# Cross-attention on one core: where the third part of product 5 is kept, and in which order GpSimd's queue takes the last batch's transfers

## The chip, the core and the metric

The kernel runs on one core of a Trainium2 chip. The core has five engines that work through their own instruction queues in order: TensorE (PE) multiplies matrices into PSUM, VectorE (DVE) adds, subtracts and scales, ScalarE (ACT) copies out of PSUM and computes exponentials, GpSimd (POOL) here reduces over the 128 partitions and issues transfers that add onto their destination, and SyncE (SP) issues plain transfers. Sixteen DMA engines carry the transfers of all queues. The metric is the device time of one execution in microseconds, as the median of a few runs; lower is better. The largest and the smallest of the runs shown lie 1.7 us apart.

## The reference

For each of 8 batches, with x1 and x2 of 512 channels by 1024 positions:

```python
q = jnp.einsum('bcn,dc->bnd', x1, Wq) + bq                # 64 wide
k = jnp.einsum('bcn,dc->bdn', x2, Wk) + bk[:, None]
v = jnp.einsum('bcn,dc->bdn', x2, Wv) + bv[:, None]
attn = jax.nn.softmax(jnp.einsum('bnd,bdm->bnm', q, k), axis=2)
attn_out = jnp.einsum('bcm,bnm->bcn', v, attn)
return attn_out + x1
```

The inputs are 32-bit floats. There is no mask: every position of x1 looks at every position of x2.

## The kernel before

The kernel does not form v. It first multiplies the unnormalised attention with x2 (stage "y"), scales by the softmax's denominators, and then multiplies with Wv (stage "o"); bv and x1 are added at the end. Both stages are products of two by two blocks, done with seven block products instead of eight. The products are numbered 1 to 7 as in the table `MULT`; their left factors are blocks or sums of blocks of x2 (`s.a`), their right factors blocks or sums of blocks of the exponentials (`s.t`: "11", "12", "21", "22", T1, T2, T3, T4). Most products of stage y are themselves done with seven smaller ones: `multiply_seeded` runs these as seven steps in the order 1, 7, 6, 2, 5, 4, 3, each of which the profile shows as four matmuls. Its steps 1, 6, 5 and 4 go through a PSUM chain (`ps_i5chain` for product 5) from which ScalarE copies into the result's banks, and step 7 makes the "third" part (`ps_i5third`), which ScalarE copies into an SBUF buffer `v` (L640). At the end `complete` adds `v` to the second bank on VectorE (L655). Which buffer `v` gets is the third argument of the call, the tag of a pool.

Tags with one buffer are shared by tiles whose lives are meant not to overlap. Two are of concern. "r" holds the output block "12" of a batch (the tile's name begins with r, as does that of block "11", which lies in "u1"), from the biased copy out of PSUM (L743) through the adding transfer of x1 onto it (L755) to the write-out (L756). "top" has two buffers used in turn. It holds the maxima over the keys of one half of the positions (L274), which VectorE subtracts before the exponential (L323); `multiply_seeded` also uses it for `v` where it is told to, and in the last batch wherever "r" is named (L633).

The program is one long list in an order written out by hand; `period(s, n, nn, nnn)` emits the work of batch `s`, interwoven with the scores, maxima and exponentials of the next batch `n` and the projections of the one after, `nn`. Batches are counted from 0 in the code. Batches 2 to 5 are "six" batches (`s.six`), with product 6 done in seven steps too; batches 1, 6 and 7 are not, and batch 0 has a branch of its own. In the last batch `n` is None.

In batches from 1 on the order of the stretch touched by the change is: product 1, VectorE's sums T1 and T2, two adding transfers that make T3 in place, the leaving of the previous batch's last outputs (x1 added by a GpSimd-issued transfer, then SyncE's write-out), product 2, the sum over half 1 (`total_1`: VectorE sums, GpSimd's reduction over partitions L293, a small transfer `few`), the eviction of y11, the inverse of half 0's denominators. In batches 1, 6 and 7 follow T4 = T2 - T21 (`copy_t4`: ScalarE negates; `add_t4`: two transfers on GpSimd's queue add T2), then product 6, in the not-last batches the next batch's scores and the queries of the one after, and product 5 with the eviction of the queries (`evict_q`) hooked behind its step 6. `shares(s, 1)` sends half 1's inverse denominators: a reciprocal on VectorE, a small transfer `row` to DRAM (L303), and a transfer that spreads it over the partitions (L308), both on GpSimd's queue. Products 7, 3 and 4 follow; product 4 reads T4, first through `inner_right` (L526 to L533), then through TensorE.

Batch 6 leaves two outputs for batch 7 to send: block "22" in the buffer "u5" and block "12" in "r". Stage o of batch 7 copies its own product 5 into "u5" as well (`multiply_57`, L579 and L594).

Of the kernel before, what the change touches and what calls it, by code (L numbers as in the profile page):

```python
# [15 lines left out]
def kernel(  # L16
# [270 lines left out]
    def total_1(s):  # L287
        sum_1(s)
        reduce_total(s, 1)
# [9 lines left out]
    def invert(s, h):  # L299

        nc.vector.reciprocal(s.few[h], s.few[h])
        s.row[h] = row = dram.tile([1, H], F32, tag="row", name=f"row_{s.b}_{h}")
        nc.gpsimd.dma_start(row.rearrange("o (p f) -> (o p) f", p=P), s.few[h])  # L303

    def spread(s, h):

        s.rden[h] = s.den[h]
        nc.gpsimd.dma_start(s.rden[h], s.row[h].broadcast_to([P, H]))  # L308

    def shares(s, h):  # L310
        invert(s, h)
        spread(s, h)
# [7 lines left out]
    def lower(s, h, i):  # L320
        e = s.e[h][:, :, i, :]
        top = s.top[h].unsqueeze(1).to_broadcast([P, 2, H])
        nc.vector.tensor_tensor(e, e, top, ALU.subtract)  # L323
# [26 lines left out]
    def copy_t4(s, parts=(0, 2)):  # L350

        if parts[0] == 0:
            s.t["T4"] = sb.tile([P, MH, H], F32, tag="eT4", name=f"eT4_{s.b}")
        t4 = s.t["T4"]
        for i in parts:
            nc.scalar.mul(t4[:, i : i + 2, :], s.t["21"][:, i : i + 2, :], -1.0)

    def add_t4(s):

        t4 = s.t["T4"]  # L360
        for i in (0, 2):
            nc.gpsimd.dma_start(t4[:, i : i + 2, :], s.t["T2"][:, i : i + 2, :], accum_op=ALU.add)

    def sum_t3(s, i):

        t3 = s.t["T3"][:, i : i + 2, :]
        nc.gpsimd.dma_start(t3, s.t["22"][:, i : i + 2, :], accum_op=ALU.add)
# [6 lines left out]
    def copy_u1(s, j):  # L374
        if j == 0:
            s.tmp[1] = sb.tile([P, 2, H], F32, tag="y22" if s.six else "yT1", name=f"uy1_{s.b}")
        nc.scalar.copy(s.tmp[1][:, j, :], s.bank["a", j])
# [118 lines left out]
    def weave(*streams):  # L496

        streams = list(streams)
        while streams:
            for stream in list(streams):  # L500
                if next(stream, "end") == "end":
                    streams.remove(stream)

    def left_stream(s, i, x, tag):

        v = {f"{p + 1}{q + 1}": x[:, ts(q, MH // 2), ts(p, P)] for p in range(2) for q in range(2)}
        sums = sb.tile([P, 4, MH // 2, P], F32, tag=tag, name=f"aI{i}_{s.b}")
        s.inner[i] = v
        for z, (k, x, y, op) in enumerate(LEFT):
            v[k] = sums[:, z]  # L510
            nc.vector.tensor_tensor(v[k], v[x], v[y], op)  # L511
            yield
# [4 lines left out]
    def right_stream(s, i, x, *tags):  # L517

        half = x.shape[1] // 2
        v = {f"{q + 1}{r + 1}": x[:, ts(q, half), ts(r, H // 2)] for q in range(2) for r in range(2)}  # L520
        last = 4 // len(tags)
        shape = [P, last, half, H // 2]
        sums = [sb.tile(shape, F32, tag=t, name=f"eI{i}{t}_{s.b}") for t in tags]
        both, t2, t4 = sums[0][:, 0:2], sums[-1][:, last - 2], sums[-1][:, last - 1]
        part = x.rearrange("p (q k) (r n) -> p q k r n", q=2, r=2)
        nc.vector.tensor_tensor(  # L526
            both, part[:, :, :, 1, :], part[:, 0].rearrange("p k r n -> p r k n"), ALU.subtract
        )
        s.inner[i, "t"] = v | {"T1": both[:, 0], "T3": both[:, 1], "T2": t2, "T4": t4}
        yield  # L530
        nc.vector.tensor_tensor(t2, both[:, 0], v["22"], ALU.subtract)
        yield
        nc.vector.tensor_tensor(t4, v["21"], t2, ALU.add)  # L533
        yield

    def inner_right(s, i, x, *tags):
        weave(right_stream(s, i, x, *tags))
# [83 lines left out]
    def multiply_seeded(s, i, v_tag, hooks={}, bank=None):  # L621

        bank = bank or MULT[i][2]

        def fresh(j):
            s.bank[bank, j] = ps = ps_a.tile(
                [P, H], F32, tag=f"{bank}{j}", name=f"ps_y{bank}{j}_{s.b}_{i}"
            )
            return ps

        b0 = fresh(0)
        chain, third = inner_parts(s, i)
        if v_tag == "top" or s.b == B - 1 and v_tag == "r":  # L633
            v = sb.tile([P, H], F32, tag="top", name=f"v{i}_{s.b}", bufs=2)[:, left]
        else:
            v = sb.tile([P, 2, H], F32, tag=v_tag, name=f"v{i}_{s.b}")[:, 0, left]
        def step(z, ps, opens, out=None, of=None):
            inner_product(s, i, z, ps, opens)
            if out is not None:
                nc.scalar.copy(out, of)  # L640
            if z in hooks:
                hooks[z]()

        step(1, chain, True, b0[:, left], chain)
        step(7, third, True, v, third)
        b1 = fresh(1)
        step(6, chain, False, b1[:, left], chain)
        step(2, b0[:, left], False)
        step(5, chain, False, b0[:, right], chain)
        step(4, b1[:, left], False, b1[:, right], chain)  # L650
        step(3, b0[:, right], False)

        def complete(b1=b1):
            b = b1.rearrange("p (a n) -> p a n", a=2)
            nc.vector.tensor_tensor(b, b, v.unsqueeze(1).to_broadcast([P, 2, H // 2]), ALU.add)  # L655

        return complete
# [249 lines left out]
    def period(s, n, nn, nnn):  # L907

        late = s.b >= 1
        five = late and nn is not None  # L910

        def first(i, rows=range(2)):
            multiply(s, "y", i, s.a, s.t, MH, rows=rows)
# [19 lines left out]
        def scores_0():  # L933
            then = scores_and(n, 0, 1 if nn else 2, "c", next_queries if nn else nothing)
            if nn is None:
                first(6, (1,))
            if s.six:
                copy_u6(s, 0)
                copy_u6(s, 1)
                nc.gpsimd.dma_start(s.tmp[6], s.tmp[1], accum_op=ALU.add)  # L940
                add_t4(s)
                weave(folds(n, 0, "max", ALU.max), right_stream(s, 7, s.t["T3"], "yT1", "yT2"))
                highest(n, 0)
            elif s.b:
                weave(folds(n, 0, "max", ALU.max), right_stream(s, 7, s.t["T3"], "yT1", "yT2"))
                highest(n, 0)
            return then
# [70 lines left out]
        else:  # L1018
# [11 lines left out]
            if not early:  # L1030
                sum_t3(s, 0)
                sum_t3(s, 2)
            for leave in s.leave:
                leave()
            if n and not early:
                invert(s, 0)
            if s.six:
# [4 lines left out]
            if n is None:  # L1042
                weave(left_stream(s, 7, s.a["S3"], "yT4"))
            complete_2 = multiply_seeded(
                s, 2, "yT1" if s.six else "y22", {5: lambda: copy_u1(s, 0), 4: lambda: copy_u1(s, 1)}
            )
            if s.b > 1:
                total_1(s)
            complete_2()
# [5 lines left out]
            if s.six:  # L1055
                complete_6 = multiply_seeded(
                    s, 6, "top", {6: lambda: copy_t4(s, (0,)), 4: lambda: copy_t4(s, (2,))}
                )
            else:
                copy_t4(s)  # L1060
                add_t4(s)
                first(6, (0,) if n and nn is None else range(2))
            if n:
                weave(left_stream(s, 7, s.a["S3"], "yT4"))
# [6 lines left out]
            if n:  # L1071
                evict_q = scores_0()
                spread(s, 0)
            if n is None:
                weave(right_stream(s, 7, s.t["T3"], "yT1", "yT2"), left_stream(s, 3, s.a["S4"], "aI3"))
            complete_5 = multiply_seeded(
                s, 5, "r", {6: evict_q} if five else {}, "a"
            )
            complete_5()
            shares(s, 1)  # L1080
            if n:
                weave(right_stream(s, 3, s.t["22"], "eT1"), left_stream(s, 3, s.a["S4"], "aI3"))
                lower(n, 0, 0)
            else:
                inner_right(s, 3, s.t["22"], "eT1")
# [160 lines left out]
        leave = evict_o(s, "22")  # L1246
# [35 lines left out]
    with tc.manual_schedule():  # L1282
        head(states[0])
        for b in range(B):
            period(*states[b : b + 4])
# [31 lines left out]
```

## Time and profile before

| what | value |
|---|---|
| median of 3 runs | 682.67 us (682.05 to 683.75) |
| the profiled execution, its time | 684.36 us |
| the profiled execution, its span | 682.6 us |
| mean granted TensorE clock in it | 0.995 of full |
| packets on the DMA engines | 134.79 MB, mean 197 GB/s |

The span is the time from the first to the last instruction that the profile shows; the profiled execution takes 1.76 us more around it. All times within the run are counted from the start of the span. A timeline row has its start, the time it covers, the engine, the line of the kernel, the operation, the tiles (out<-in), their size and the count; in brackets stands the idle time of the engine before it and what ended it. A row of the list of waits has the total, the number of times and the longest.

### The profile page before, as it was taken

How to read it: one execution, taken by the hardware profiler on the slowest of the kernel's cores; microseconds unless marked ns; L12 is line 12 of the kernel's file. 1: busy time of each engine (PE TensorE's matmuls, PEld its weight loads, DVE VectorE, ACT ScalarE, POOL GpSimd, SP SyncE). 2: the span in 40 equal slices, each digit the busy share in tenths (PEclk: the TensorE clock that was granted, in tenths of full speed). 3: DMA queues.
4: the chain of work that ended last, by engine and by line, in shares of the span. 5: the costliest groups of instructions: out<-in, count | busy, mean ns of one | idle time of the engine just before them, and what ended most of it. 6: DMA issues, size and time to landing. Idle time of an engine off the chain costs nothing.

```text
span 682.6 us, 7705 instructions
## 1 busy us (share of the span) xinstructions
PE 668.1 (98%) x2558; PEld 425.3 (62%) x2558; DVE 607.1 (89%) x823; ACT 363.4 (53%) x636; POOL 226.8 (33%) x196
## 2 busy tenths in 40 slices
PE   9999999979999999999999999999999999999997
PEld 5334754737557685586656876566855767566854
DVE  1998899895989899897999989998999989989894
ACT  2754466424754556645655557556476346564321
POOL 0126214631145413443224631354223540145400
PEclk9999999997999999999999999999999999999999
DMA  9678587995499897998699985999959991688602
GB/s 300 270 204 266 164 232 139 196 238 182 108 254 217 191 262 187 225 208 224 189 252 207 220 229 163 276 200 224 261 102 210 196 311 49 123 139 187 154 31 108
DMA packets 51783, 134.79 MB, mean 197 GB/s; under 512 B 5664, under 2 KB 7968, under 8 KB 51744
## 3 DMA queue, kind: packets, MB, share of 16 engines
q0 software_dynamic: 24480, 61.94, 50.2%
q1 hardware_dynamic: 26976, 71.97, 29.6%
q10 hardware_dynamic: 288, 0.39, 0.2%
q8 instruction: 20, 0.33, 0.2%
q14 instruction: 19, 0.16, 0.1%
HBM read 86.77 MB, written 16.81 MB: 152 GB/s over the span
## 4 chain that ended last, share of the span: by engine, by line
PE 78%; DMA 11%; DVE 4%; POOL 2%; issue 2%; ACT 2%; SPq 0%; DVEq 0%; POOLq 0%; ACTq 0%
PE ps_yc L544 9%; PE ps_ya L544 6%; PE ps_s L238 5%; PE ps_oa L463 5%; PE ps_oa L585 5%; PE ps_o L463 4%; PE ps_o L483 4%; PE ps_oc L463 4%; PE ps_k L191 3%; PE ps_i4chain L544 3%; PE ps_q L191 3%; PE ps_i3chain L544 2%; DMA uo<-in_x_dram 2%; PE ps_i5chain L544 2%; PE ps_i7chain L544 2%
## 5 line engine op out<-in xcount | busy, mean ns | idle before, releaser
L293 POOL PARTITION_ALL_REDUCE den<-sum x16 | 53.4, 3340 | 75.9 <-DVE sum L268 75.9
L763 POOL DMA_DIRECT2D sum<-e x21 | 26.9, 1279 | 140.5 <-ACT sum L768 43.6
L323 DVE TENSOR_TENSOR e<-e,top 128x1024 f32<-128x1024 f32 x60 | 71.4, 1217 | 2.3 <-POOL top L274 2.3
L332 ACT ACTIVATE e<-e 128x1024 f32<-128x1024 f32 x60 | 62.7, 1056 | 12.1 <-DVE e L323 11.4
L274 POOL PARTITION_ALL_REDUCE top<-max x16 | 32.2, 2012 | 64.0 <-DVE max L268 42.4
L247 ACT COPY e<-ps_s 128x1024 f32<-128x1024 f32 x46 | 45.6, 1029 | 9.7 <-PE ps_s L238 7.0
L238 PE MATMUL ps_s<-q,k 64*128 64x512 f32 x188 | 47.6, 608 | 0.9 <-ACT q L790 0.8
L258 DVE TENSOR_TENSOR max<-max,e 128x1024 f32<-128x1024 f32 x30 | 36.5, 1216 | 0.2
L238 PEld LDWEIGHTS ps_s<-q,k 64*128 64x128 f32 x188 | 17.3, 186 | 22.5 <-issue 15.5
L640 ACT COPY ps_ya<-ps_i1chain 128x256 f32<-128x256 f32 x28 | 10.0, 358 | 36.9 <-PE ps_i1chain L544 33.4
L677 DVE TENSOR_TENSOR y<-y,den 128x1024 f32<-128x1024 f32 x24 | 29.2, 1234 | 0.2
L308 POOL DMA_DIRECT2D den<-row x16 | 8.9, 558 | 60.9 <-DMA row<-few 40.9
L755 POOL DMA_DIRECT2D r<-in_x_dram x14 | 28.5, 2033 | 1.0 <-ACT ps_yc L640 1.0
L463 PE MATMUL ps_oa<-yT,w_S 128*128 128x512 f32 x64 | 28.8, 592 | 0.0
L463 PE MATMUL ps_o<-y,w 128*128 128x512 f32 x64 | 28.8, 592 | 0.0
L483 PE MATMUL ps_o<-y,w 128*128 128x512 f32 x64 | 28.8, 592 | 0.0
L463 PE MATMUL ps_oc<-yT,w 128*128 128x512 f32 x64 | 28.8, 592 | 0.0
L640 ACT COPY ps_yc<-ps_i7chain 128x256 f32<-128x256 f32 x32 | 11.4, 357 | 31.2 <-PE ps_i7chain L544 25.2
L511 DVE TENSOR_TENSOR aI<-a,aI 128x256 f32<-128x256 f32 x60 | 25.2, 421 | 1.3
L640 ACT COPY ps_ya<-ps_i5chain 128x256 f32<-128x256 f32 x32 | 11.4, 358 | 27.8 <-PE ps_i5chain L544 22.9
L511 DVE TENSOR_TENSOR aI<-a 128x256 f32<-128x256 f32 x60 | 25.7, 449 | 0.0
L191 PE MATMUL ps_q<-x_in_x_dram,wqk_sb 128*64 128x512 f32 x112 | 25.6, 598 | 0.0
(282 smaller groups left out, 1788.4 us busy)
## 6 DMA issues: line engine op xcount, KB each, us to landing
x_in_x_dram<-in_x_dram SPq DMA_DIRECT2D x60, 512.0 KB, 8.9
a<-in_x2T_dram SPq DMA_DIRECT2D x32, 512.0 KB, 10.3
sum<-e POOLq DMA_DIRECT2D x21, 512.0 KB, 7.5
aS<-in_x2T_dram POOLq DMA_DIRECT2D x19, 512.0 KB, 10.4
eT<-eT POOLq DMA_DIRECT2D x16, 512.0 KB, 11.1
uo<-in_x_dram POOLq DMA_DIRECT2D x14, 512.0 KB, 10.1
r<-in_x_dram POOLq DMA_DIRECT2D x14, 512.0 KB, 11.3
e<-e POOLq DMA_DIRECT2D x14, 512.0 KB, 10.8
```

Of the source, the lines that this page charges most:

```text
L191: nc.tensor.matmul(ps[r, :], w_sb[:, c, :], s.x[:, c, ts(h, H)], start=(c == 0), stop=(c == CT - 1),)
L238: nc.tensor.matmul(ps[g], s.k[r, ts(i, P)], s.q[r, ts(h, H)], start=True, stop=True)
L247: nc.scalar.copy(e[:, :, i, :], whole)
L258: nc.vector.tensor_tensor(f, e[:, :, 0, :] if i == 1 else f, e[:, :, i, :], op)
L293: nc.gpsimd.partition_all_reduce(s.den[h], s.mx[h][:, 0, :], P, ReduceOp.add)
L323: nc.vector.tensor_tensor(e, e, top, ALU.subtract)
L332: nc.scalar.activation(e, e, AF.Exp)
L463: nc.tensor.matmul(ps[:, n], left[ka][:, k, ts(j, P)], right[kb][:, k, n], start=opens and k == 0, stop=i in (2, 3, 4) and k == n_k - 1, s ...
L483: nc.tensor.matmul(ps, w["11"][:, k, ts(j, P)], s.y["11"][:, k, :], start=k == 0, stop=False, skip_group_check=True)
L511: nc.vector.tensor_tensor(v[k], v[x], v[y], op)
L544: nc.tensor.matmul(ps, s.inner[i][ka][:, k, :], s.inner[i, "t"][kb][:, k, :], start=opens and k == 0, stop=z in (2, 3, 4) and k == n_k - 1 ...
L585: nc.tensor.matmul(ps[:, n], w[ka][:, k, ts(j, P)], s.y[kb][:, k, n], start=False, stop=i == 3 and k == 1, skip_group_check=True,)
```

## The change

Three edits. The third part of product 5 goes to the buffer tag "top" in the batches that are not "six" batches (1, 6 and 7; the last used "top" already). In the last batch, the negations and transfers of T4 are put between product 2 and the sum over half 1. And in the last batch the leaving of batch 6's outputs (both the transfers of x1 onto them and the write-outs) is put behind the sending of half 1's denominators.

```diff
-            for leave in s.leave:
-                leave()
+            if n:
+                for leave in s.leave:
+                    leave()
             if n and not early:
                 invert(s, 0)
...
             complete_2 = multiply_seeded(
                 s, 2, "yT1" if s.six else "y22", {5: lambda: copy_u1(s, 0), 4: lambda: copy_u1(s, 1)}
             )
+            if n is None:
+                copy_t4(s)
+                add_t4(s)
             if s.b > 1:
                 total_1(s)
...
             else:
-                copy_t4(s)
-                add_t4(s)
+                if n:
+                    copy_t4(s)
+                    add_t4(s)
                 first(6, (0,) if n and nn is None else range(2))
...
             complete_5 = multiply_seeded(
-                s, 5, "r", {6: evict_q} if five else {}, "a"
+                s, 5, "r" if s.six else "top", {6: evict_q} if five else {}, "a"
             )
             complete_5()
             shares(s, 1)
+            if n is None:
+                for leave in s.leave:
+                    leave()
```

The order of instructions changes on GpSimd's queue alone. In batch 7, behind the two transfers of T3, it was: x1 onto "u5", x1 onto "r", the reduction of half 1, `few` of half 1, `row` and the spread of half 0, T4's two transfers, `row` and the spread of half 1. It becomes: T4's two transfers, the reduction of half 1, `few` of half 1, `row` and the spread of half 0, `row` and the spread of half 1, x1 onto "u5", x1 onto "r". SyncE's write-outs keep their places, and wait for the x1 transfers as before.

## The prediction

> Batches are counted from 0 here, as in the code, so the title's batches 2 and 7 are batches 1 and 6, and the last is batch 7. Times within the run are microseconds of the profiled execution before the change.
>
> **What bounds the kernel now.** First the page's table of engines, then the list of what TensorE's matmuls waited for.
>
> ```profile
> PE 668.1 (98%) x2558; PEld 425.3 (62%) x2558; DVE 607.1 (89%) x823; ACT 363.4 (53%) x636; POOL 226.8 (33%) x196
> ```
> ```profile
> PE ps_i5chain L544 <- ACT ps_ya L640: 5.5, 1, 5.5
> ...
> PE ps_i4third L544 <- DVE eI4eT L526: 1.0, 1, 1.0
> ```
>
> TensorE (PE) is busy for 668.1 of 682.6 us, so the end moves only if TensorE waits less or runs faster. Inside the batches it has one long pause, before a step of product 5, and one of 1.0 us before a step of product 4. The timeline shows what each costs. The first three rows below are product 5 of batch 1 (its first step, the step behind the pause, the second step of product 7); the last two are the same first step and the same second step of product 7 in batch 6, which has no pause.
>
> ```profile
> 145.90 1.13 PE L544 MATMUL ps_i5chain<-eT,aS 128*128 128x256 f32 x4
> ...
> 155.08 2.08 PE L544 MATMUL ps_i5chain<-eI5y,aI 128*128 128x256 f32 x4 [5.46 <-ACT ps_ya L640]
> ...
> 161.44 1.03 PE L544 MATMUL ps_i7third<-eI7yT,aI 128*128 128x256 f32 x4
> ```
> ```profile
> 556.26 1.03 PE L544 MATMUL ps_i5chain<-eT,aS 128*128 128x256 f32 x4
> ...
> 563.16 1.03 PE L544 MATMUL ps_i7third<-eI7yT,aI 128*128 128x256 f32 x4
> ```
>
> The same eight steps take 161.44 - 145.90 = 15.54 us in batch 1 and 563.16 - 556.26 = 6.90 us in batch 6 (0.86 a step). The excess is 8.64 us, of which 5.46 is the pause; the rest, 3.18, is a slower clock, as the 2 us windows show (their first number after POOL's is the granted clock, the next the DMA engines' busy share).
>
> ```profile
> 154.00:156.00 2.00, 0.92 (x2) 0.84 (x3) 0.00 (x0) 1.60 (x4) 0.79 (x2) 0.50 1.03 394
> ...
> 160.00:162.00 2.00, 2.00 (x9) 1.69 (x8) 1.46 (x3) 0.31 (x1) 0.54 (x1) 0.80 0.91 213
> ...
> 164.00:166.00 2.00, 2.00 (x11) 1.74 (x11) 1.60 (x3) 0.40 (x2) 0.54 (x1) 1.00 0.00 0
> ...
> 174.00:176.00 2.00, 2.00 (x12) 0.77 (x8) 2.00 (x5) 2.00 (x3) 0.00 (x0) 1.00 0.00 0
> ```
>
> Behind the pause the clock is at half until somewhere past 160. Who made the pause stands on ScalarE (ACT) and on SyncE's queue (SP):
>
> ```profile
> 145.87 0.37 SPq L756 DMA_DIRECT2D out_dram<-r  x1
> ```
> ```profile
> 154.38 0.37 ACT L640 COPY v<-ps_i5third 128x256 f32<-128x256 f32 x1 [6.90 <-DMA out_dram<-r]
> ...
> 168.55 0.37 ACT L640 COPY v<-ps_i3third 128x256 f32<-128x256 f32 x1 [0.45 <-PE ps_i3third L544]
> ```
>
> The copy of product 5's third part waits 6.90 us, because its buffer "r" is still being written out for batch 0, a transfer issued at 145.87. ScalarE's later copies stand behind it in order, and TensorE needs those.
>
> **The change, part by part.** *Product 5 in batch 1.* The part goes to "top", the two buffers of the maxima, used in turn. The copy then takes the buffer of batch 1's maximum of half 1, and has to wait for that maximum alone, the first row below; the second is the next maximum, in the other buffer.
>
> ```profile
> 107.86 2.20 POOL L274 PARTITION_ALL_REDUCE top<-max  x1
> ...
> 144.17 4.13 POOL L293 PARTITION_ALL_REDUCE den<-sum  x1 [8.31 <-DVE sum L268]
> ...
> 152.57 1.77 POOL L274 PARTITION_ALL_REDUCE top<-max  x1 [3.38 <-DVE max L268]
> ```
>
> So it needs no wait: pause and half clock both go, **-8.64 us** (bounds: 5.46 if the clock were low anyway, 8.64). What becomes late next? Product 3's third part stays in "r" and inherits the wait. It stood at 168.55 and moves to 168.55 - 8.64 = 159.91; the write-out had landed by 154.38, 5.5 us earlier, so this costs nothing. The transfers in flight at the pause are over by 164 (DMA share 0.00), before the next keys' matmuls need their x at 176.39 - 8.64 = 167.75:
>
> ```profile
> 176.39 3.65 PE L191 MATMUL ps_k<-x_in_x_dram,wqk_sb 128*64 128x512 f32 x16
> ```
>
> VectorE (DVE) waited in this pause too, and its work now falls beside GpSimd's maximum at 152.57:
>
> ```profile
> 145.12 3.26 DVE L526 TENSOR_TENSOR eI7yT<-e 128x1024 f32<-128x1024 f32 x1
> ...
> 159.28 0.70 DVE L655 TENSOR_TENSOR ps_ya<-ps_ya,v 128x512 f32<-128x512 f32 x1 [6.82 <-ACT ps_ya L640]
> ...
> 160.60 1.22 DVE L526 TENSOR_TENSOR eI3eT<-e 128x1024 f32<-128x1024 f32 x1 [0.54 <-PE ps_ya L544]
> ```
>
> The form that takes 1.22 us took 3.26 beside GpSimd's sum at 144.17, so such company can cost 2.04. VectorE is free at 159.28 - 6.82 = 152.46; the first sum for product 3 starts 0.78 behind it (160.60 - 159.28, less the 0.54 idle) and takes 1.22, so it is ready by 154.5, or 156.5 with the 2.04 added. Product 3's second step, which reads it, starts one step ahead of its copy, 159.91 - 0.86 = 159.05. I take 0 (bounds 0 and 2.04). The Trainium skill, page "SBUF — State Buffer", section "SBUF: two separate sides", speaks against this change here: VectorE operations with two SBUF inputs and GpSimd exclude each other for the whole instruction. That would make the 2.04 likely, and still leave it covered by the slack just worked out.
>
> *Product 5 in batch 6* copies without waiting for the write-out already (the steps above run at 0.86), so 0; bounds 0 and 0.
>
> *The last batch.* T4 is -T21 by ScalarE plus T2 by a transfer. Before, the two transfers stand in GpSimd's queue behind half 1's sum, and behind the sending of half 0's denominators.
>
> ```profile
> 623.41 2.00 ACT L356 ACTIVATE eT<-e 128x1024 f32<-128x1024 f32 x2
> ```
> ```profile
> 620.84 1.85 POOL L755 DMA_DIRECT2D uo<-in_x_dram  x1
> ...
> 630.35 3.23 POOL L293 PARTITION_ALL_REDUCE den<-sum  x1 [6.44 <-DVE sum L268]
> ...
> 637.85 1.85 POOL L362 DMA_DIRECT2D eT<-eT  x2
> ```
> ```profile
> 637.99 0.17 DVE L301 RECIPROCAL few<-few 128x4 f32<-128x4 f32 x1
> ...
> 646.96 1.23 DVE L526 TENSOR_TENSOR eI4eT<-eT 128x1024 f32<-128x1024 f32 x1 [1.25 <-DMA eT<-eT]
> ```
> ```profile
> 646.32 1.03 PE L544 MATMUL ps_i4chain<-eT,a 128*128 128x256 f32 x4
> 648.33 1.10 PE L544 MATMUL ps_i4third<-eI4eT,aI 128*128 128x256 f32 x4 [0.98 <-DVE eI4eT L526]
> ```
>
> After, they wait for the negations, over at 623.41 + 2.00 = 625.41, and their two issues (1.85) are off GpSimd by 627.3, 3 us before the sum can start: the sum is not delayed, so bounds 0 and 0. Their landing, from the view of their line, is:
>
> ```profile
> L362 POOL DMA_DIRECT2D eT<-eT x16: 919/1250/2121, 62.7 to 638.4; - x16
> ...
> DMA to landing us min/median/max: 5.6/11.1/18.1
> ```
>
> Even 18.1 from the last issue (about 626.5) gives 644.6, ahead of VectorE's 646.96 - 1.25 = 645.71. VectorE gains 1.25, and TensorE's second step of product 4 starts at 646.32 + 0.86 = 647.18 instead of 648.33: **-1.15 us**. VectorE's chain to the end keeps its distance, since it moves by slightly more. Bounds 0 and 1.15.
>
> *The two x1 transfers onto batch 6's outputs* move from 620.84 past half 1's sum, both denominators' rows and both spreads, to GpSimd's last place; SyncE's two write-outs follow them, with batch 7's write-outs queued behind. The reader to fear is "u5": batch 7's own part of product 5 is copied into it.
>
> ```profile
> 665.80 0.59 ACT L594 COPY uo<-ps_oc 128x512 f32<-128x512 f32 x1 [4.56 <-PE ps_oc L585]
> ```
> ```profile
> DMA to landing us min/median/max: 1.7/6.7/14.1
> ```
> ```profile
> DMA to landing us min/median/max: 6.4/11.7/16.3
> ```
> ```profile
> DMA to landing us min/median/max: 2.7/8.5/11.2
> ```
>
> These three rows belong to the denominators' row (L303), the x1 transfers (L755) and the write-outs (L756). From the reciprocal's end at 638.16, with 0.55 for an issue, an empty machine gives 638.16 + 1.7 + 0.55 + 6.4 + 2.7 = 649.5, the medians 665.6, the maxima 680.3. The copy stands at 665.80 - 1.15 = 664.65. The medians come from a machine mostly loaded; here T4 is out of the way. In this stretch the rows were:
>
> ```profile
> uo<-in_x_dram POOLq DMA_DIRECT2D x1, 512.0 KB, 9.9
> ...
> out_dram<-uo SPq DMA_DIRECT2D x1, 512.0 KB, 3.8
> ```
>
> With the median row, 638.16 + 6.7 + 0.55 + 9.9 + 3.8 = 659.1: 5 us in hand. I take 0 (bounds 0 and 15.7 of lateness).
>
> **The sum:** 8.64 + 0 + 1.15 + 0 = 9.79 us. The span falls from 682.6 to 672.8; the median of the runs shown, 682.67, is 0.07 above this span, so 672.9.
>
> The Trainium skill, page "TensorE: Matmul & The Clock Gate", section "Part 1: The HAM clock gate", puts the half clock after a pause at about 3.4 us of work, which loses 1.7; the windows lose 3.18. An estimate by that page is 5.46 + 1.7 + 1.15 = 8.3 and 674.4 us. The measurement counts.
>
> **Rivals.** *(a) The pause comes back in batch 2,* whose product 5 still uses "r":
>
> ```profile
> 228.08 0.37 SPq L756 DMA_DIRECT2D out_dram<-r  x1
> ```
> ```profile
> 237.22 0.37 ACT L640 COPY v<-ps_i5third 128x256 f32<-128x256 f32 x1 [0.45 <-PE ps_i5third L544]
> ```
>
> At the median landing of 8.5 that write-out ends at 236.6, 0.6 us before the copy. If the transfers are what sets its time, the copy moving 8.64 forward waits 8.0, and TensorE gets back about the old pause: 682.67 - 1.15 = 681.5. For it: little slack. Against it: the DMA share is 0.00 at 164 and at 174, so no backlog is carried over, and what follows is started by the engines that have moved. 4%.
>
> *(b) The edit does not free the copy,* because it must wait for the younger maximum, which ends at 154.34, as late as the write-out: 681.5 again. Against it is the turn of the two buffers. 3%.
>
> *(c) Only the idle time is saved,* the clock being low there for another reason: 682.67 - 5.46 - 1.15 = 676.1. The clock is full in every other window I read, so 5%.
>
> *(d) Slower:* the last batch's copy into "u5" waits for batch 6's write-out. At the maxima it is 680.3 - 664.65 = 15.7 us late with TensorE behind it, and the clock loses another 3.18: 672.9 + 18.9 = 691.8. It makes the whole slower than before from a write-out that lands some 6.6 us past 664.65, about 671.3 (9.79 less 3.18). Against it: the DMA engines have only these two transfers and one spread to carry. 4%.
>
> **How the numbers follow.** The forecast has 84%. About 0.3%, 2 us, is what a measurement here tells from no change. Forecast and (c) are faster: 89%; (a) and (b) are within: 7%; (d) slower: 4%. The range starts at 671.6, about 0.2% of scatter below the forecast (the three runs spread from 682.05 to 683.75), and goes to 676.6, which takes in (c), the skill's estimate, a lock of 2.04 that is not hidden, and the medians' lateness of 1.0 at "u5"; some 15% lies outside.
>
> **What would show it.** Right: no wait of the copy of product 5's third part on a write-out in batch 1, eight steps there in 6.9 us at full clock, the copy of product 3 unhindered, product 4's second step in batch 7 right behind its first. Wrong: a TensorE pause in batch 2's product 5 (a), in batch 1 at the younger maximum (b), half clock without a pause (c), or a copy into "u5" in batch 7 waiting for a write-out (d).

## The result, and the profile after

| | median | runs |
|---|---|---|
| before | 683.09 us | 682.05 to 683.75, 4 runs |
| after | 673.40 us | 672.73 to 674.69, 4 runs |

The ratio is 0.9862, 95% interval 0.9841 to 0.9882: the change takes 9.7 us off. A second comparison (label f3_again below) gave 0.9866, 0.9852 to 0.9880. The profiled execution after has a span of 671.0 us.

The page's table of engines and its line of granted clocks, after:

```profile
PE 663.4 (99%) x2558; PEld 423.0 (63%) x2558; DVE 606.4 (90%) x823; ACT 363.4 (54%) x636; POOL 226.7 (34%) x196
...
PEclk9999999999999999999999999999999999999999
```

TensorE is 4.7 us less busy with the same 2558 matmuls; some 3 us of that is the half clock of batch 1, which shows in none of the 40 slices any more. The list of TensorE's waits, after, whole:

```profile
PE ps_warm L835 <- DVE warm L832: 1.0, 1, 1.0
PE ps_s L238 <- ACT q L790: 0.8, 1, 0.8
PE ps_ya L463 <- ACT e L318: 0.3, 1, 0.3
PE ps_q L786 <- DMA x_head<-in_x_dram: 0.2, 1, 0.2
```

Both waits shown of before are gone, and what is left lies outside the stretches that the change touches. The timeline of product 5 in batch 1, TensorE and ScalarE, after:

```profile
144.66 1.13 PE L544 MATMUL ps_i5chain<-eT,aS 128*128 128x256 f32 x4
...
148.22 1.03 PE L544 MATMUL ps_i5chain<-eI5y,aI 128*128 128x256 f32 x4
...
151.67 1.03 PE L544 MATMUL ps_i7third<-eI7yT,aI 128*128 128x256 f32 x4
...
157.71 1.03 PE L544 MATMUL ps_i3third<-eI3eT,aI 128*128 128x256 f32 x4
```
```profile
146.75 0.37 ACT L640 COPY v<-ps_i5third 128x256 f32<-128x256 f32 x1 [0.51 <-PE ps_i5third L544]
...
158.78 0.37 ACT L640 COPY v<-ps_i3third 128x256 f32<-128x256 f32 x1 [0.45 <-PE ps_i3third L544]
```

The third part's copy waits for its matmuls alone. The step that the pause stood before comes without one, and the eight steps take 151.67 - 144.66 = 7.01 us. Product 3's third part, still in "r", waits for nothing else either. The last batch, on GpSimd, TensorE, SyncE's queue and ScalarE, after:

```profile
614.37 1.79 POOL L362 DMA_DIRECT2D eT<-eT  x2 [3.30 <-DVE aI L511]
619.72 3.23 POOL L293 PARTITION_ALL_REDUCE den<-sum  x1 [3.56 <-DVE sum L268]
...
630.39 0.54 POOL L308 DMA_DIRECT2D den<-row  x1 [2.02 <-issue]
630.93 1.26 POOL L755 DMA_DIRECT2D uo<-in_x_dram  x1
```
```profile
635.93 1.03 PE L544 MATMUL ps_i4chain<-eT,a 128*128 128x256 f32 x4
636.79 1.03 PE L544 MATMUL ps_i4third<-eI4eT,aI 128*128 128x256 f32 x4
```
```profile
637.17 0.37 SPq L756 DMA_DIRECT2D out_dram<-uo  x1
```
```profile
654.19 0.59 ACT L594 COPY uo<-ps_oc 128x512 f32<-128x512 f32 x1 [4.56 <-PE ps_oc L585]
```

T4's transfers are off GpSimd 3.6 us before the sum, product 4's second step follows its first in 0.86 us, and the copy into "u5" waits for its matmuls, as before.

Where the 11.6 us between the two spans lie, by the same rows of both kernels:

| stretch | before | after | difference |
|---|---|---|---|
| start to product 5 of batch 1 | 145.90 | 144.66 | -1.24 |
| its eight steps | 15.54 | 7.01 | -8.53 |
| then to product 4 of batch 7 | 484.88 | 484.26 | -0.62 |
| its first step | 2.01 | 0.86 | -1.15 |
| then to the end | 34.27 | 34.21 | -0.06 |

The two stretches with the change hold 9.68 us, about what the medians moved by (9.69; the ratio makes it 9.4). The other 1.9 us come from stretches whose instructions are the same; single executions of one kernel differ by about as much.

### The profile page after: what moved, and what is told of

It reads as the page before. It is cut to its first block, busy times and chain, and to the rows that moved or that the text cites. A ratio compares the mean times of both kernels' runs of the same rounds, so it can differ in the third digit from the quotient of the medians.

```text
span 671.0 us, 7705 instructions
## 1 busy us (share of the span) xinstructions
PE 663.4 (99%) x2558; PEld 423.0 (63%) x2558; DVE 606.4 (90%) x823; ACT 363.4 (54%) x636; POOL 226.7 (34%) x196
## 4 chain that ended last, share of the span: by engine, by line
PE 93%; DMA 4%; DVE 1%; SPq 1%; ACT 0%; issue 0%; POOL 0%; DVEq 0%; ACTq 0%
PE ps_yc L544 12%; PE ps_ya L544 7%; PE ps_s L238 6%; PE ps_oa L585 6%; PE ps_oa L463 5%; PE ps_ya L463 4%; PE ps_oc L463 4%; PE ps_o L463 4%; PE ps_o L483 4%; PE ps_q L191 4%; PE ps_i5chain L544 3%; PE ps_k L191 3%; PE ps_i4chain L544 3%; PE ps_i3chain L544 3%; PE ps_i7chain L544 3%; PE ps_i2chain L544 3%
## 5 line engine op out<-in xcount | busy, mean ns | idle before, releaser
L755 POOL DMA_DIRECT2D r<-in_x_dram x14 | 26.9, 1922 | 1.6 <-ACT ps_yc L640 1.0
## 6 DMA issues: line engine op xcount, KB each, us to landing
eT<-eT POOLq DMA_DIRECT2D x16, 512.0 KB, 11.6
```

## The experiments

Every time is compared with the kernel before on the same chip in the same comparison; its medians there were 682.1 to 682.7 us.

### The parts of the change, one at a time

**e1_top_only, and f4_top_again: only "top".**

```diff
-                s, 5, "r", {6: evict_q} if five else {}, "a"
+                s, 5, "r" if s.six else "top", {6: evict_q} if five else {}, "a"
```

> Product 5's third part in "top" in batches 1 and 6, the last batch as before. Theory (the pause and the half clock of batch 1 are the write-out's doing): eight steps of product 5 in batch 1 in 6.9 us instead of 15.5, no pause; 682.7 - 8.6 = 674.1 us; the 1.0 us pause of product 4 in batch 7 stays. Rival (the copy meets another wait, or the DMA engines take the gain back in batch 2): about 681.5 us, with a pause of over 4 us in batch 1 or 2.

Measured: 676.12 us, ratio 0.9934 (0.9908 to 0.9961), with the runs far apart: six of ten between 673.3 and 676.2, four between 680.0 and 682.1. The profiled one took 680.48. In it the pause on "r" is gone, but another stands some 10 us ahead of it. VectorE's timeline, TensorE's, and a window of that execution:

```profile
139.49 0.69 DVE L531 TENSOR_TENSOR eI5u<-eI5y,eT 128x512 f32<-128x512 f32 x1 [7.10 <-DMA out_dram<-r]
```
```profile
142.71 2.67 PE L238 MATMUL ps_sc<-q,k 64*128 64x512 f32 x4 [4.13 <-DVE y L691]
```
```profile
144.00:146.00 2.00, 2.00 (x6) 1.24 (x5) 1.97 (x4) 1.17 (x2) 0.00 (x0) 0.50 1.06 220
```

VectorE's second sum for product 5's right side goes to the buffer "u1", from which batch 0's block 11 is still being written out (its tile's name begins with r too). It waits 7.10 us there; the eviction of y11, behind it in VectorE's order, is late, and TensorE's scores need the banks that it frees: 4.13 us of pause, and half clock behind it. Before the change such an execution would next have met the pause on "r", which ends with a write-out whenever TensorE gets there, and would have lost little more; that is argued here, and tried with f2_u1_only below. In the profile of the changed kernel VectorE did not wait here. T4's wait, which was expected to stay, is small in this execution (0.31 us of VectorE; TensorE's list of waits has none). The same kernel in another comparison:

> The kernel with only "top" changed, once more, likely on another chip. Theory (its first runs, 673.3 to 682.1, met a long wait on "u1", 7.1 us in the profile, which the same kernel need not meet elsewhere): without a long wait 673.4 + 1.15 = 674.5 us, runs within 673 to 676.5; with it, the same spread, and again a wait of VectorE for block 11's write-out of 5 us or more in the profile of a run near 680. Rival (the spread has another cause): the spread with a short wait, or none.

Measured: 675.85 us, ratio 0.9903 (0.9889 to 0.9916), five runs from 675.4 to 676.8. VectorE's wait is short there, and the profile shows two small waits besides, the first VectorE's, the second TensorE's:

```profile
134.51 0.69 DVE L531 TENSOR_TENSOR eI5u<-eI5y,eT 128x512 f32<-128x512 f32 x1 [2.25 <-DMA out_dram<-r]
154.39 0.18 DVE L301 RECIPROCAL few<-few 128x4 f32<-128x4 f32 x1 [2.54 <-DMA few<-den]
```
```profile
161.16 1.13 PE L544 MATMUL ps_i3chain<-eI3eT,aI 128*128 128x256 f32 x4 [0.67 <-ACT ps_yc L640]
640.14 1.10 PE L544 MATMUL ps_i4third<-eI4eT,aI 128*128 128x256 f32 x4 [1.13 <-DVE eI4eT L526]
```

The pause of T4 stays, as it should. The median lies 1.3 us above the expected 674.5. The 0.67 is a part of that, and a second wait of a step of product 3, 0.70 us in batch 3 (0.36 in the profile before), may be another. That the other runs above 680 had the long wait too is likely, not shown: one of them was profiled.

**e2_top_b6: "top" in batch 6 alone.**

```diff
-                s, 5, "r", {6: evict_q} if five else {}, "a"
+                s, 5, "top" if s.b == 6 else "r", {6: evict_q} if five else {}, "a"
```

> The same edit in batch 6 alone. Theory: no wait stood there, so no change: 682.7 us, the 5.5 us pause in batch 1 as before. Rival (batch 6 has a hidden share of the gain): below 682 by more than the interval.

Measured: 682.05 us, ratio 0.9993 (0.9983 to 1.0003), the pause of 5.5 us in batch 1 in place. Batch 6's edit brings nothing that can be measured. Its profile shows something else, in TensorE's rows of product 5 in batch 1 and in the windows around the half clock:

```profile
144.68 1.13 PE L544 MATMUL ps_i5chain<-eT,aS 128*128 128x256 f32 x4
...
153.85 2.07 PE L544 MATMUL ps_i5chain<-eI5y,aI 128*128 128x256 f32 x4 [5.46 <-ACT ps_ya L640]
...
159.23 1.03 PE L544 MATMUL ps_i7third<-eI7yT,aI 128*128 128x256 f32 x4
```
```profile
150.00:152.00 2.00, 0.00 (x0) 0.00 (x0) 1.24 (x3) 0.00 (x0) 0.65 (x1) 0.69 1.06 375
...
156.00:158.00 2.00, 2.00 (x7) 1.59 (x7) 0.00 (x0) 0.65 (x2) 0.00 (x0) 0.60 1.05 341
```

The pause is as long as before, but the clock falls earlier in it, and the eight steps take 159.23 - 144.68 = 14.55 us: 5.46 of pause and 2.19 of clock, not 3.18. The last section comes back to this.

**e3_last_only: the last batch alone.** Against the changed kernel:

```diff
-                s, 5, "r" if s.six else "top", {6: evict_q} if five else {}, "a"
+                s, 5, "r", {6: evict_q} if five else {}, "a"
```

> The two edits of the last batch alone. Theory: product 4's second step in batch 7 right behind its first, 1.15 us less: 681.5 us; the pause of batch 1 stays. Rival (the x1 transfers behind cost what T4 brings): 682.7 us with a wait of the copy into "u5" in batch 7, or a later denominator.

Measured: 681.28 us, ratio 0.9986 (0.9978 to 0.9995), that is 1.0 us off, 0.3 to 1.5. In its profile the wait of product 4's second step is gone, and the pause of 5.5 us in batch 1 is there. The theory holds.

**e4_t4_only: T4 ahead, the x1 transfers where they were.**

```diff
             complete_2 = multiply_seeded(
...
+            if n is None:
+                copy_t4(s)
+                add_t4(s)
             if s.b > 1:
                 total_1(s)
...
             else:
-                copy_t4(s)
-                add_t4(s)
+                if n:
+                    copy_t4(s)
+                    add_t4(s)
```

> In the last batch T4's negations and transfers ahead of half 1's sum, the x1 transfers where they were, ahead of T4; product 5 as before. Theory (T4 was late by its place behind the sum and the spread): T4's issue at about 625, its landing below 643 although it shares the DMA engines with x1, no wait of VectorE for it: 681.5 us, the same as with both edits. Rival (the x1 transfers were what held T4 up): the wait for T4 stays at 1 us or more, 682.7 us.

Measured: 682.83 us, ratio 1.0017 (1.0007 to 1.0027): a loss of 0.5 to 1.8 us. VectorE does not wait for T4, as expected, but it waits elsewhere. Its timeline and TensorE's:

```profile
637.19 0.18 DVE L301 RECIPROCAL few<-few 128x4 f32<-128x4 f32 x1 [1.94 <-DMA few<-den]
```
```profile
645.86 1.10 PE L544 MATMUL ps_i4third<-eI4eT,aI 128*128 128x256 f32 x4 [0.52 <-ACT ps_ya L640]
```

The small transfer `few` of half 1 is now behind six large ones that add (T3, x1 and T4), lands 6.1 us after its issue (2.0 in e3_last_only), and holds up the reciprocal and with it VectorE's sums for products 3 and 4. From product 5's first step to product 4's second TensorE takes 20.52 us here, against 20.14 before and 18.99 in e3_last_only: T4's wait is gone, and the wait for `few` has taken its place. The profiled execution, 681.89 us, is the fastest of the ten; it shows some 0.4 us of the measured loss, and the rest is not shown. The second half of the edit, which looks like mere tidying, is what makes the first half pay.

**e5_x1_only: the x1 transfers behind, T4 where it was.**

```diff
-            for leave in s.leave:
-                leave()
+            if n:
+                for leave in s.leave:
+                    leave()
...
             shares(s, 1)
+            if n is None:
+                for leave in s.leave:
+                    leave()
```

> In the last batch the x1 transfers behind everything, T4 in its old place behind half 1's sum and half 0's spread; product 5 as before. Theory: T4 is issued at 637.9 as before, and as before no x1 transfer is in flight then, so the wait for it stays near 1.2 us: 682.7 us. Rival (x1 was what held T4 up): the wait is gone, 681.5 us.

Measured: 681.97 us, ratio 0.9997 (0.9983 to 1.0012). VectorE's wait for T4 is smaller, and not gone:

```profile
644.66 1.23 DVE L526 TENSOR_TENSOR eI4eT<-eT 128x1024 f32<-128x1024 f32 x1 [0.74 <-DMA eT<-eT]
```

TensorE still waits 0.48 us at product 4's second step. So T4 was late by its place in the queue mainly, and moving the x1 transfers alone is no remedy that can be measured.

### Is the half clock the pause's doing?

**e7_fill: work in the pause.**

```diff
         step(2, b0[:, left], False)
+        if i == 5 and s.b == 1:
+            spare = ps_a.tile([P, H], F32, tag="c1", name="ps_fill")
+            for _ in range(6):
+                nc.tensor.matmul(spare, s.a["S1"][:, 0, 0:P], s.t["T1"][:, 0, :], start=True, stop=True)
         step(5, chain, False, b0[:, right], chain)
```

> The kernel before, with six more 128x512 matmuls on TensorE in batch 1's product 5, between its steps 2 and 5, into a PSUM bank that nobody reads: 6 x 0.86 = 5.2 us of work inside the 5.46 us pause. Theory (the half clock is the pause's doing): no half clock behind it, the wait on the write-out unchanged, 682.7 - 3.2 = 679.5 us. Rival (the clock is low there for another reason): half clock as before and 682.7 us or more.

Measured: 678.61 us, ratio 0.9953 (0.9941 to 0.9965): 3.5 us less with more work. The timelines of TensorE and ScalarE, and the window behind the filling:

```profile
148.02 5.31 PE L652 MATMUL ps_fill<-eT,aS 128*128 128x512 f32 x12
153.62 1.13 PE L544 MATMUL ps_i5chain<-eI5y,aI 128*128 128x256 f32 x4 [0.29 <-ACT ps_ya L640]
...
157.18 1.03 PE L544 MATMUL ps_i7third<-eI7yT,aI 128*128 128x256 f32 x4
```
```profile
152.92 0.37 ACT L640 COPY v<-ps_i5third 128x256 f32<-128x256 f32 x1 [6.88 <-DMA out_dram<-r]
```
```profile
154.00:156.00 2.00, 2.00 (x11) 1.73 (x10) 0.00 (x0) 1.55 (x4) 0.00 (x0) 1.00 1.04 410
```

ScalarE waits 6.88 us for the write-out, as before. The clock stays full, and the steps behind take 157.18 - 153.62 = 3.56 us instead of 161.44 - 155.08 = 6.36. The half clock was the pause's doing.

**e6_r_first: a shorter pause.**

```diff
-            for leave in s.leave:
+            for leave in s.leave[::-1] if s.b == 1 else s.leave:
                 leave()
```

> The kernel before, with batch 0's block 12 (buffer "r") sent ahead of its block 22 in batch 1: x1 onto it and its write-out each go first. Theory: the write-out of "r" is issued at 143.3 instead of 145.9 and lands some 2.6 us sooner; the pause of TensorE shrinks from 5.5 to about 2.9 us. If the clock falls behind so short a pause too, 682.7 - 2.6 = 680.1 us; if it does not, 682.7 - 2.6 - 3.2 = 676.9 us. Rival (the pause is not set by that write-out): pause and time unchanged.

Measured: 680.03 us, ratio 0.9974 (0.9963 to 0.9985).

```profile
144.85 1.13 PE L544 MATMUL ps_i5chain<-eT,aS 128*128 128x256 f32 x4
...
152.00 2.07 PE L544 MATMUL ps_i5chain<-eI5y,aI 128*128 128x256 f32 x4 [3.43 <-ACT ps_ya L640]
...
158.30 1.03 PE L544 MATMUL ps_i7third<-eI7yT,aI 128*128 128x256 f32 x4
```
```profile
154.00:156.00 2.00, 2.00 (x7) 1.55 (x6) 0.00 (x0) 0.55 (x2) 0.00 (x0) 0.50 1.02 365
156.00:158.00 2.00, 2.00 (x7) 1.67 (x6) 1.26 (x3) 0.17 (x1) 0.54 (x1) 0.60 1.05 369
```

The pause shrinks with the write-out, to 3.43 us, and the clock falls all the same. The eight steps take 13.45 us, 6.55 more than the 6.90 of batch 6: 3.43 of pause and 3.12 of clock.

### When do the x1 transfers come too late?

**e8_x1_late.** In the changed kernel, behind the eviction of y21:

```diff
+        if n is None:
+            late_sb = const.tile([P, 1], F32, name="late_sb")
+            nc.gpsimd.tensor_copy(late_sb, s.y["21"][:, 1, H - 1 : H])
+            for leave in s.leave:
+                leave()
```

> The changed kernel, with the two x1 transfers of the last batch held until VectorE has evicted y21 (a one-column copy on GpSimd waits for it): issued at about 646 instead of 631. Theory (the copy into "u5" waits for the write-out and nothing else does): x1 lands 6.2 us after its issue, the write-out 3.9 after that, so about 656.5, some 2.3 us behind the copy's 654.2; TensorE pauses by about 2 us less what it has in hand: 673.4 + 1 to 2, up to 3.2 more if the clock falls: 674.4 to 678.6 us. Rival (the order of these transfers has no bearing on the end): 673.4 us.

Measured: 676.15 us, ratio 0.9923 (0.9898 to 0.9948); the changed kernel has 673.4.

```profile
656.80 0.58 ACT L594 COPY uo<-ps_oc 128x512 f32<-128x512 f32 x1 [7.28 <-DMA out_dram<-uo]
```
```profile
657.71 0.70 PE L544 MATMUL ps_io7chain<-eIo7eT,w_I 128*128 128x256 f32 x2 [1.94 <-ACT ps_oa L553]
```
```profile
655.00:660.00 5.00, 3.06 (x11) 1.66 (x10) 0.00 (x0) 1.78 (x5) 0.00 (x0) 1.00 0.79 300
```

The copy starts at 656.80 (expected 656.5); 4.56 of the 7.28 us it waits in the changed kernel too. TensorE pauses 1.94 us, and the clock does not fall. The mechanism of rival (d) is real; the change keeps clear of it.

### The wait that is left

**f3_again: the changed kernel in another comparison.**

> The changed kernel again, in more rounds. Up to the last batch it is the same program as the one with only "top" changed, whose runs went from 673.3 to 682.1. Theory (VectorE's wait for batch 0's block 11 to leave "u1" comes and goes from run to run, and "r" no longer covers it): the runs spread here too, from about 672.5 (no wait) to about 680 (a wait of 7 us with TensorE pausing and half clock behind it), median 673 to 677. Rival (that spread belonged to the other kernel or to the chip): all within 672.5 to 675.

Measured: 673.28 us, ratio 0.9866 (0.9852 to 0.9880), runs from 672.5 to 674.3. The rival's spread, then. VectorE's wait on "u1" is 2.27 us in its profile, and the long one did not come up. But the short one has a price here, as in f4_top_again; VectorE's rows and TensorE's:

```profile
134.51 0.69 DVE L531 TENSOR_TENSOR eI5u<-eI5y,eT 128x512 f32<-128x512 f32 x1 [2.27 <-DMA out_dram<-r]
154.44 0.18 DVE L301 RECIPROCAL few<-few 128x4 f32<-128x4 f32 x1 [2.59 <-DMA few<-den]
```
```profile
161.22 1.13 PE L544 MATMUL ps_i3chain<-eI3eT,aI 128*128 128x256 f32 x4 [0.74 <-ACT ps_yc L640]
```

In batch 1 the sum over half 1 stands behind product 5's right sums in VectorE's order (not ahead of them, as the description of the other batches has it). So a wait on "u1" makes the sum and its transfer `few` late, the reciprocal waits for `few`, the sums for product 3 follow it, and TensorE pauses 0.74 us.

**f1_free_u1: "u1" freed in the changed kernel.**

```diff
-                right_stream(s, 5, s.t["T1"], "u5" if s.six else "y21", "u1"),
+                right_stream(s, 5, s.t["T1"], "u5" if s.six else "y21", "aI3" if s.b == 1 else "u1"),
```

> The changed kernel, with the second part of product 5's right sums in batch 1 in "aI3", free there, instead of "u1". Theory (the spread is the wait on "u1"): VectorE waits for no write-out in batch 1 and the runs close up at the fast end, 672 to 674.7, median near 673. Rival: the spread stays.

Measured in the same comparison: 672.37 us, ratio 0.9852 (0.9839 to 0.9865), runs from 672.0 to 672.8, the lowest of all kernels here. VectorE waits for no write-out in batch 1, its reciprocal waits for nothing, and TensorE's 0.74 us in product 3 are gone. The intervals of the two ratios overlap, so the 0.9 us over the changed kernel is not sure. The four runs lie within 0.8 us, those of the changed kernel within 1.8, as the theory has it, though so few runs do not show it.

**f2_u1_only: the same edit in the kernel before.**

> The kernel before, with that second part in "aI3" in batch 1 and nothing else. Theory (before, the wait on "r" stands behind the one on "u1" and covers it whatever its length): 682.1 us, as before, the pause on "r" as long or longer. Rival (the wait on "u1" cost time before as well): under 681 us.

Measured: 683.04 us, ratio 1.0007 (0.9997 to 1.0018). Before, freeing "u1" gains nothing: the pause on "r" (5.6 us in its profile) covers the wait of some 2.3 us that the kernel before shows. No profile of that kernel caught the long wait, so that the pause covers 7 us too stays argued.

## Why the prediction was right

**The pause in batch 1.** The forecast had 8.64 us for it and the profiles show 8.53; e1_top_only and f4_top_again show that "top" alone brings most of the gain (ratios of 0.9934 and 0.9903, by which 4.5 and 6.6 us), and e2_top_b6 that batch 6 brings none that can be measured. Both parts of the sum, the pause and the clock behind it, are real, which rules out (c): e7_fill gets the second part back with the pause left alone. That the size agrees to 0.1 us is in part luck. In the six profiles that have the pause on "r" at its full length (5.2 to 5.7 us: before, e2 to e5 and f2_u1_only) the eight steps take from 14.37 to 15.84 us, because the part lost to the clock goes from 2.2 to 3.4. The forecast took it from one of them.

**What was said to become late next.** Product 3's copy found "r" free. Batch 2 did not take the gain back (a): its write-out of "r" is issued at 218.23, before at 228.08, and the copy stands at 227.45, before at 237.22; they moved by 9.85 and 9.77. The maximum did not hold the copy (b). One step of the working was wrong without changing the sum: the first sum for product 3 was to be ready by 154.5, on the ground that VectorE's order had nothing else to wait for. VectorE's timeline after:

```profile
152.73 0.18 DVE L301 RECIPROCAL few<-few 128x4 f32<-128x4 f32 x1 [1.49 <-DMA few<-den]
152.82 1.20 DVE L526 TENSOR_TENSOR eI3eT<-e 128x1024 f32<-128x1024 f32 x1
```

The reciprocal ahead of it waits for the landing of `few`, which the old pause had hidden. It is done at 154.0, which on a clock that began 1.24 us earlier is some 0.8 late, and product 3's step reads it at 157.71: covered in this execution. It is not always: where VectorE had waited some 2.3 us on "u1" as well, the reciprocal's wait was 2.5 to 2.6 and TensorE lost 0.74 (f3_again, the same kernel) and 0.67 (f4_top_again). The term that the forecast put at 0, with 2.04 as its bound, is 0 to 0.7 us, and for another reason than GpSimd's company. The lock beside GpSimd was not put to the test: GpSimd's maximum ran from 150.01 to 151.78, over before that sum began, which took 1.20.

**The last batch.** 1.15 us were forecast and the two profiles show 1.15; e3_last_only measures 1.0 (0.3 to 1.5). That the profiles agree so well is again in part luck: from product 5's first step to product 4's second TensorE takes 18.99 us in every profile with both moves (after, e3_last_only, e8_x1_late, f1_free_u1, f3_again), but without them 20.14 before, 19.01 in e7_fill, 19.22 in e1_top_only and 20.37 in f2_u1_only. What T4's place costs varies from 0.0 to 1.4 us between executions. The forecast treated the two moves as a gain from T4 and a zero from x1. By e4_t4_only the zero is wrong taken alone: without x1's move, T4's costs 1.2 us net (0.5 to 1.8), because `few` is then behind six adding transfers. The sum is right, since both moves are in the change.

**The x1 transfers and "u5" (d).** The estimate put the write-out's landing at 659.1, 5 us ahead of the copy. After, it is issued at 637.17 and lands 3.9 us later, 13 us ahead: the denominators' row took 2.0 us and not the median's 6.7, and x1 took 6.2 and not 9.9. Before, each stood just behind two large adding transfers in GpSimd's queue (T4's and T3's), and now neither does; that this is the reason is likely, not shown.

**What the forecast missed** is the wait on "u1". The profile before shows it, 2.29 us of VectorE at 135.73, and its price in TensorE's time was zero there. That it varies between executions (from 0 to 7.1 us in these profiles), that the pause on "r" had covered it, and that behind the change 2.3 us of it cost TensorE 0.7, stands in none of the rivals. What makes it 7.1 us is open; the write-out took 9.7 us to land in that execution, and 5.1 in f3_again.

## What to carry to other kernels

A pause that ends with a transfer, whenever the engine gets there, can hide shorter waits ahead of it; when it is removed, look upstream for waits that the trace prices at zero, not only downstream. A buffer that is being written out is a poor place for a copy that an in-order engine must make, and a buffer with an idle twin is better; the price of a pause of TensorE is its length plus the slow clock behind it, here 2.2 to 3.4 us, so one profile does not give it to better than 1 us. And where transfers are moved ahead in a queue, count the small ones that now stand behind them.

## What the runs showed of the hardware

The half clock lasts 6.8 us wherever these profiles show it, and what of that falls into the pause itself costs nothing. The table has where it begins and ends (from the windows at the two edges, each taken as part full and part half clock), how much of it TensorE is at work, and what the eight steps of product 5 lose beyond the pause (their time, less 6.90 us and the pause).

| profile | pause | half clock | of it at work | lost |
|---|---|---|---|---|
| before | 5.46 | 154.0 to 160.8 | 5.7 | 3.18 |
| e6_r_first | 3.43 | 150.8 to 157.6 | 5.6 | 3.12 |
| e2_top_b6 | 5.46 | 150.8 to 157.6 | 3.7 | 2.19 |
| f2_u1_only | 5.57 | 153.3 to 160.1 | 6.1 | 3.37 |

So a shorter pause is not a cheaper clock (e6_r_first against before), and pauses of one length differ by a microsecond (e2_top_b6 against before): it hangs on how far into the pause the clock falls, from 2.2 us behind TensorE's last matmul in e6_r_first to 4.8 in f2_u1_only. What sets that moment these runs do not show. The Trainium skill, page "TensorE: Matmul & The Clock Gate", section "Part 1: The HAM clock gate", has about 3.4 us of work until the clock is full again; by the windows it is 3.7 to 6.1 us here, and the windows decide. The same section has the clock fall after an idle window of about 3.4 us; the lengths of the pauses agree, since it fell in those of 3.43, 4.13 and about 5.5 us and not in those of 1.94 or 0.98, but the fall itself came as early as 2.2 us into a pause.
